# Taking the variances of a four-layer graph network from ScalarE squares, and starting the last six batches ahead

## The chip, the cores and the metric

The kernel runs on one core of one Trainium2 chip. The metric is the device time of one execution in microseconds (us). Before the change the median of the first three runs is 3364.07 us (3363.28 to 3366.58).

Short names: PE is TensorE's matmuls, PEld its weight loads, DVE is VectorE, ACT is ScalarE, POOL is GpSimd. "L198" is line 198 of the kernel in question; the change shifts most lines by 3 to 16, so one operation has two numbers (the product is L195 before and L198 after; query-key matmuls are L442 and L445, value products' transposing matmuls L619 and L629, the copy of their result oT L628 and L638). prT is the result of layer 3's softmax, written to DRAM (p_d) by one DMA transfer and read back, rearranged, by another; "half clock" is a granted TensorE clock of 0.50 in a stretch.

## The reference, cut to what matters

Four layers run over 128 independent batches, each a 128 x 512 tile. Each layer ends in a residual addition and a normalisation, and layer 3 has one more normalisation inside, so that a batch has five:

```python
def _layernorm(x, axis=-1, eps=1e-5):
    m = jnp.mean(x, axis=axis, keepdims=True)
    v = jnp.var(x, axis=axis, keepdims=True)
    return (x - m) / jnp.sqrt(v + eps)

x = _layernorm(x + adj @ x @ W0 + bias0)                       # layer 0
x = _layernorm(x + elu(softmax(e(x)) @ (x @ W1) + beta * ...)) # layer 1, masked graph attention
x = _layernorm(x + max over neighbours(...))                   # layer 2
# layer 3: 8 heads of masked attention, o = attention @ w_proj + b_proj
ln = (o - mu) * rsqrt(var + eps) * gamma + beta
x = _layernorm(x + o + ln)
```

The four lines for the layers are abbreviated; `_layernorm` is the reference's own.

## The kernel before

All instructions are issued by one program in a static order. A class `Plan` decides that order when the kernel is built: each batch is a chain of steps, each step names its engine and an assumed duration, and the plan always issues next the step that could start earliest by its own bookkeeping. Ties go to urgent steps, then to the lower rank. On the chip every engine worked through its queue in that order: in the trace of this kernel the 2304 instructions of ScalarE, the 5263 of VectorE and the 1027 of GpSimd start in the order of the built program, line for line, and so do PE's 1045 runs of matmuls of one line.

```python
    def use(self, engine, work, take=None, late=0.05, urgent=False):
        names = take if callable(take) else lambda: (take,) if take else ()
        return engine, work, names, late, not urgent
    ...
    def run(self):
        while self.requests:
            t, _, _, n = min(
                (self.at(r), r["want"][4], r["rank"], n) for n, r in enumerate(self.requests)
            )
            ...
            self.free[engine] = t + work
            self.now = r["ready"] = t + work + late
```

The normalisation takes mean and variance on VectorE, and 1/sqrt as a power on GpSimd:

```python
    def mean_rstd(src):
        yield use("DVE", 1.0)
        st = small.tile([P, 6], F32, name="st")
        nc.vector.bn_stats(st, src)
        mv = small.tile([P, 2], F32, name="mv")
        nc.vector.bn_aggr(mv, st)
        ve = small.tile([P, 1], F32, name="ve")
        nc.vector.tensor_scalar(ve, mv[:, 1:2], EPS, None, op0=ALU.add)
        yield use("POOL", 0.65, late=0.1, urgent=True)
        rstd = small.tile([P, 1], F32, name="rstd")
        nc.gpsimd.tensor_tensor(rstd, ve, neghalf, op=ALU.pow)
        return mv, rstd
```

The end of a batch's layer 3, and the ranks:

```python
        yield use("ACT", 0.6, urgent=True)
        oT = buf([P, K, P], "oT")
        nc.scalar.copy(oT, p)
        give(ba)
        bp = yield use("PE", 3.5, "mm", late=0.2)
        p = product(lambda k: oT[:, k, :], lambda k: wproj_sb[:, k, :])
        give(bo)
        bo = yield use("DVE", 0.69, "o", urgent=True)
        o = buf([P, D], "o")
        nc.vector.tensor_tensor(o, p, bproj_sb, op=ALU.add)
        give(bp)
        yield biased
        added = Event()
        plan.start(pool_add(xb, o, added), i)      # xb += o on GpSimd
        mv, rstd = yield from mean_rstd(o)
        yield added
        yield use("DVE", 1.65)
        ...                                        # two multiply-adds on DVE
        yield from layernorm_dve(xb)
        ...
        for i in range(NB):
            plan.start(batch(i), i if i < NB - 4 else i - 16)
        plan.run()
```

So the last four of the 128 batches run 16 ranks ahead, and others end the kernel.

## Time and profile before

| | before |
|---|---|
| median of three runs | 3364.07 us |
| profiled span | 3366.0 us |
| PE busy | 3324.6 us (99%) |
| DVE / ACT busy | 2669.9 / 1189.7 us (79% / 35%) |
| PE idle in the first 200 us | 7.9 us |
| PE idle from 200 to 3000 us | 7.7 us |

A busy time is the union of an engine's instructions. The last two rows are a stretch's length less PE's busy time in it. The granted TensorE clock was 1.00 from 200 to 3000 us. The profile's lines are in the prediction below; where they show a bracket such as `[5.99 <-DMA prT<-p_d]`, the engine was idle for 5.99 us before the instruction, until the named transfer landed.

### The profile page before, as it was taken

How to read it: one execution, taken by the hardware profiler on the slowest of the kernel's cores; microseconds unless marked ns; L12 is line 12 of the kernel's file. 1: busy time of each engine (PE TensorE's matmuls, PEld its weight loads, DVE VectorE, ACT ScalarE, POOL GpSimd, SP SyncE). 2: the span in 40 equal slices, each digit the busy share in tenths (PEclk: the TensorE clock that was granted, in tenths of full speed). 3: DMA queues.
4: the chain of work that ended last, by engine and by line, in shares of the span. 5: the costliest groups of instructions: out<-in, count | busy, mean ns of one | idle time of the engine just before them, and what ended most of it. 6: DMA issues, size and time to landing. Idle time of an engine off the chain costs nothing.

```text
span 3366.0 us, 43501 instructions
## 1 busy us (share of the span) xinstructions
PE 3324.6 (99%) x14729; PEld 2070.5 (62%) x14729; DVE 2669.9 (79%) x5527; ACT 1189.7 (35%) x3457; POOL 923.1 (27%) x1031
## 2 busy tenths in 40 slices
PE   9999999999999999999999999999999999999987
PEld 5665656566565666566656656665656665666655
DVE  7878786886978878877877886887887787788775
ACT  3433333333233334343333333333333333333332
POOL 2322221331322312312322331232232232232221
PEclk9999999999999999999999999999999999999999
DMA  4332323223232323222232322232322323232222
GB/s 157 98 103 63 104 75 93 69 80 113 68 99 76 97 79 91 94 79 82 79 109 66 100 85 91 85 89 83 91 85 82 98 73 97 76 94 88 69 82 75
DMA packets 458191, 296.01 MB, mean 88 GB/s; under 512 B 315888, under 2 KB 389744, under 8 KB 457968
## 3 DMA queue, kind: packets, MB, share of 16 engines
q1 hardware_dynamic: 457968, 293.23, 29.0%
q8 instruction: 117, 1.92, 0.2%
q14 instruction: 106, 0.87, 0.1%
HBM read 150.54 MB, written 142.61 MB: 87 GB/s over the span
## 4 chain that ended last, share of the span: by engine, by line
PE 90%; DVE 6%; DMA 2%; issue 1%; SPq 0%; ACT 0%; POOL 0%; POOLq 0%; DVEq 0%; ACTq 0%
PE mm L195 47%; PE mm L442 27%; PE tr L203 6%; PE sc L572 4%; PE tr L619 4%; PE mm L543 3%; DVE st L161 1%; DMA p_d<-pt 1%; DMA prT<-p_d 1%; DVE scr L516 1%; DVE x L648 1%; PE tr L383 0%; SPq L486 0%; DVE t L645 0%; DVE x L182 0%
## 5 line engine op out<-in xcount | busy, mean ns | idle before, releaser
L442 PE MATMUL mm<-xT,wqkv_sb 128*128 128x256 f32 x4096 | 918.2, 381 | 8.8 <-DVE st L161 8.8
L195 PE MATMUL mm<-w_sb,yT 128*128 128x512 f32 x2048 | 913.9, 596 | 2.3 <-ACT yT L206 2.3
L442 PEld LDWEIGHTS mm<-xT,wqkv_sb 128*128 128x128 f32 x4096 | 771.4, 190 | 138.3 <-issue 20.6
L168 POOL TENSOR_TENSOR rstd<-ve,neghalf 128x1 f32<-128x1 f32 x640 | 406.6, 635 | 1100.6 <-DVE ve L165 996.9
L195 PEld LDWEIGHTS mm<-w_sb,yT 128*128 128x128 f32 x2048 | 383.3, 191 | 453.3 <-issue 441.6
L188 POOL TENSOR_TENSOR x<-x,o 128x512 f32<-128x512 f32 x128 | 175.9, 1374 | 1128.3 <-DVE o L636 1117.6
L195 PE MATMUL mm<-wqkv_sb,xT 128*128 128x512 f32 x1024 | 464.4, 596 | 0.0
L195 PE MATMUL mm<-wproj_sb,oT 128*128 128x512 f32 x1024 | 460.9, 598 | 1.8 <-ACT oT L628 1.8
L590 ACT ACTIVATE pr<-pr,nmx 128x128 f32<-128x128 f32 x1024 | 397.6, 391 | 176.1 <-DVE nmx L586 174.6
L161 DVE BATCH_NORM_STATS2 st<-x 128x6 f32<-128x512 f32 x512 | 348.1, 680 | 3.1 <-ACT x L550 1.9
L579 DVE TENSOR_TENSOR pr<-sc,maskb 128x1024 f32<-128x1024 f32 x128 | 156.3, 1221 | 218.8 <-PE sc L572 218.0
L195 PEld LDWEIGHTS mm<-wproj_sb,oT 128*128 128x128 f32 x1024 | 191.8, 191 | 223.6 <-issue 214.4
L177 ACT ACTIVATE x<-x,nmr,rstd 128x512 f32<-128x512 f32 x256 | 205.0, 810 | 351.6 <-DVE nmr L175 326.9
L195 PEld LDWEIGHTS mm<-wqkv_sb,xT 128*128 128x128 f32 x1024 | 189.6, 190 | 199.0 <-issue 191.4
L206 ACT COPY yT<-tr 128x512 f32<-128x512 f32 x256 | 146.8, 582 | 263.9 <-PE tr L203 263.6
L188 POOL TENSOR_TENSOR x<-x,beta_sb 128x512 f32<-128x512 f32 x128 | 167.1, 1307 | 177.1 <-DVE xt L556 131.2
L516 DVE SCALAR_TENSOR_TENSOR scr<-x,wa_rows 128x512 f32<-128x512 f32 x256 | 200.4, 783 | 15.5 <-ACT x L177 10.2
L468 ACT COPY v<-mm 128x512 f32<-128x512 f32 x128 | 74.9, 585 | 347.7 <-PE mm L195 347.5
L450 ACT ACTIVATE qkT<-mm 128x512 f32<-128x512 f32 x128 | 76.1, 594 | 341.2 <-PE mm L442 341.0
L590 ACT ACTIVATION_READ_ACCUMULATOR pr<-pr,nmx 128x1 f32 x1024 | 193.1, 189 | 0.0
L188 POOL TENSOR_TENSOR x<-x,bias_sb 128x512 f32<-128x512 f32 x128 | 182.6, 1436 | 32.9 <-PE tr L203 22.9
L182 DVE TENSOR_SCALAR x<-x,mv,rstd 128x512 f32<-128x512 f32 x256 | 172.5, 676 | 14.4 <-POOL rstd L168 14.0
(63 smaller groups left out, 3558.6 us busy)
## 6 DMA issues: line engine op xcount, KB each, us to landing
p_d<-pt SPq DMA_DIRECT2D x128, 512.0 KB, 2.6
prT<-p_d SPq DMA_DIRECT2D x128, 512.0 KB, 3.8
x<-in_x SPq DMA_DIRECT2D x128, 256.0 KB, 2.9
x_d<-xt SPq DMA_DIRECT2D x128, 256.0 KB, 2.0
xT<-x_d SPq DMA_DIRECT2D x512, 64.0 KB, 2.5
out<-x SPq DMA_DIRECT2D x128, 256.0 KB, 2.0
e_d<-et SPq DMA_DIRECT2D x64, 128.0 KB, 1.7
eT<-e_d SPq DMA_DIRECT2D x64, 128.0 KB, 2.2
```

Source lines behind the costliest of these rows:

```text
L161: nc.vector.bn_stats(st, src)
L168: nc.gpsimd.tensor_tensor(rstd, ve, neghalf, op=ALU.pow)
L177: nc.scalar.activation(xb, xb, AF.Identity, bias=nmr, scale=rstd)
L182: nc.vector.tensor_scalar(xb, xb, mv[:, 0:1], rstd, op0=ALU.subtract, op1=ALU.mult)
L188: nc.gpsimd.tensor_tensor(dst, dst, other, op=ALU.add)
L195: nc.tensor.matmul(p, lhs(k), rhs(k), start=(k == 0), stop=(k == K - 1))
L203: nc.tensor.matmul(p[:, k, :], xb[:, k * P : (k + 1) * P], nodes, start=True, stop=True)
L206: nc.scalar.copy(yT, p)
L442: nc.tensor.matmul(p[:, j, :], wqkv_sb[:, k, (c + j) * P : (c + j + 1) * P], gr.xT[:, k, :], start=(k == 0), stop=(k == K - 1),)
L516: nc.vector.scalar_tensor_tensor(scr, xb, 1.0, wa_rows[:, j, :], op0=ALU.mult, op1=ALU.mult, accum_out=gr.s[:, b, j : j + 1],)
L579: nc.vector.tensor_tensor(pr, sc.rearrange("p j c m -> p (j c) m"), maskb[:, None, :].to_broadcast([P, H, P]), op=ALU.add,)
L590: nc.scalar.activation(pr[:, j, :], pr[:, j, :], AF.Exp, bias=nmx[:, j : j + 1], accum_out=sums[:, j : j + 1],)
```

## The change

The intent is to move the variance of all 640 normalisations from VectorE to ScalarE, which had two thirds of its time free (35% busy). The sum of a row now comes from an accumulator of the operation that writes the row, VectorE makes the negated mean of it, ScalarE squares the row about that mean and accumulates. Besides, six last batches run 12 ranks ahead, in place of four by 16. Cut to its core:

```diff
-    def mean_rstd(src):
-        yield use("DVE", 1.0)
-        st = small.tile([P, 6], F32, name="st")
-        nc.vector.bn_stats(st, src)
-        mv = small.tile([P, 2], F32, name="mv")
-        nc.vector.bn_aggr(mv, st)
+    def mean_rstd(src, total):
+        yield use("DVE", 0.15)
+        nm = small.tile([P, 1], F32, name="nm")
+        nc.vector.tensor_scalar(nm, total, -1.0 / D, None, op0=ALU.mult)
+        yield use("ACT", 1.0)
+        square = one.tile([P, D], F32, name="square")
+        var = small.tile([P, 1], F32, name="var")
+        nc.scalar.activation(square, src, AF.Square, bias=nm, accum_out=var)
+        yield use("DVE", 0.15)
         ve = small.tile([P, 1], F32, name="ve")
-        nc.vector.tensor_scalar(ve, mv[:, 1:2], EPS, None, op0=ALU.add)
+        nc.vector.tensor_scalar(ve, var, 1.0 / D, EPS, op0=ALU.mult, op1=ALU.add)
 ...
-        nc.vector.tensor_tensor(xb, p, xb, op=ALU.add)
+        nc.vector.scalar_tensor_tensor(
+            xb, p, 1.0, xb, op0=ALU.mult, op1=ALU.add, accum_out=total
+        )
 ...   (likewise with accum_out at the other four places that write a row to be normalised)
-                plan.start(..., g * G + 2 * h - (16 if g * G >= NB - 4 else 0))
+                plan.start(..., g * G + 2 * h - (12 if g * G >= NB - 6 else 0))
 ...   (likewise for the query-key steps)
-            plan.start(batch(i), i if i < NB - 4 else i - 16)
+            plan.start(batch(i), i if i < NB - 6 else i - 12)
```

More of the change, by code (lines that the diff above doesn't have):

```diff
@@ L168, in mean_rstd, with layernorm_act, layernorm_dve @@
         nc.gpsimd.tensor_tensor(rstd, ve, neghalf, op=ALU.pow)
-        return mv, rstd
-    def layernorm_act(xb):
-        mv, rstd = yield from mean_rstd(xb)
+        return nm, rstd
+    def layernorm_act(xb, total):
+        nm, rstd = yield from mean_rstd(xb, total)
         yield use("DVE", 0.21)
         nmr = small.tile([P, 1], F32, name="nmr")
-        nc.vector.tensor_scalar(nmr, mv[:, 0:1], rstd, -1.0, op0=ALU.mult, op1=ALU.mult)
+        nc.vector.tensor_tensor(nmr, nm, rstd, op=ALU.mult)
         yield use("ACT", 0.81)
         nc.scalar.activation(xb, xb, AF.Identity, bias=nmr, scale=rstd)
-    def layernorm_dve(xb):
-        mv, rstd = yield from mean_rstd(xb)
+    def layernorm_dve(xb, total):
+        nm, rstd = yield from mean_rstd(xb, total)
         yield use("DVE", 0.67)
-        nc.vector.tensor_scalar(xb, xb, mv[:, 0:1], rstd, op0=ALU.subtract, op1=ALU.mult)
+        nc.vector.tensor_scalar(xb, xb, nm, rstd, op0=ALU.add, op1=ALU.mult)
     def pool_add(dst, other, event, after=None):
@@ L369, in group @@
             for h in range(G // 2):
-                plan.start(attention1(groups[g], h), g * G + 2 * h - (16 if g * G >= NB - 4 else 0))
+                plan.start(attention1(groups[g], h), g * G + 2 * h - (12 if g * G >= NB - 6 else 0))
             for n in range(K):
-                plan.start(query_key(groups[g], n // 2 * 2 + K * (n % 2)), g * G + n / K - (16 if g * G >= NB - 4 else 0))
+                plan.start(query_key(groups[g], n // 2 * 2 + K * (n % 2)), g * G + n / K - (12 if g * G >= NB - 6 else 0))
         return groups[g]
@@ L507, in batch @@
         yield biased
-        yield use("DVE", 0.69, urgent=True)
-        nc.vector.tensor_tensor(xb, p, xb, op=ALU.add)
+        yield use("DVE", 0.78, urgent=True)
+        total = small.tile([P, 1], F32, name="total")
+        nc.vector.scalar_tensor_tensor(
+            xb, p, 1.0, xb, op0=ALU.mult, op1=ALU.add, accum_out=total
+        )
         give(bp)
-        yield from layernorm_act(xb)
+        yield from layernorm_act(xb, total)
         yield wa_ready
@@ L532, in batch @@
         nc.scalar.activation(ex, p, AF.Exp)
-        yield use("DVE", 1.5, urgent=True)
+        yield use("DVE", 1.6, urgent=True)
+        total = small.tile([P, 1], F32, name="total")
         nc.vector.scalar_tensor_tensor(xb, p, 0.0, xb, op0=ALU.max, op1=ALU.add)
-        nc.vector.scalar_tensor_tensor(xb, ex, 1.0, xb, op0=ALU.min, op1=ALU.add)
+        nc.vector.scalar_tensor_tensor(
+            xb, ex, 1.0, xb, op0=ALU.min, op1=ALU.add, accum_out=total
+        )
         give(bp)
         give(be)
-        yield from layernorm_act(xb)
+        yield from layernorm_act(xb, total)
         bp = yield use("PE", 0.95, "mm", late=0.2, urgent=True)
@@ L548, in batch @@
         give(bp)
-        yield use("ACT", 0.81)
-        nc.scalar.activation(xb, xb, AF.Identity, bias=mx)
-        yield from layernorm_dve(xb)
+        yield use("ACT", 0.92)
+        total = small.tile([P, 1], F32, name="total")
+        nc.scalar.activation(xb, xb, AF.Identity, bias=mx, accum_out=total)
+        yield from layernorm_dve(xb, total)
         bt = yield use("DVE", 0.65, "xt")
@@ L633, in batch @@
         give(bo)
-        bo = yield use("DVE", 0.69, "o", urgent=True)
+        bo = yield use("DVE", 0.78, "o", urgent=True)
         o = buf([P, D], "o")
-        nc.vector.tensor_tensor(o, p, bproj_sb, op=ALU.add)
+        total = small.tile([P, 1], F32, name="total")
+        nc.vector.scalar_tensor_tensor(
+            o, p, 1.0, bproj_sb, op0=ALU.mult, op1=ALU.add, accum_out=total
+        )
         give(bp)
@@ L640, in batch @@
         plan.start(pool_add(xb, o, added), i)
-        mv, rstd = yield from mean_rstd(o)
+        nm, rstd = yield from mean_rstd(o, total)
         yield added
-        yield use("DVE", 1.65)
+        yield use("DVE", 1.75)
         t1 = one.tile([P, D], F32, name="t1")
         nc.vector.scalar_tensor_tensor(
-            t1, o, mv[:, 0:1], gamma_sb, op0=ALU.subtract, op1=ALU.mult
+            t1, o, nm, gamma_sb, op0=ALU.add, op1=ALU.mult
         )
-        nc.vector.scalar_tensor_tensor(xb, t1, rstd, xb, op0=ALU.mult, op1=ALU.add)
+        total = small.tile([P, 1], F32, name="total")
+        nc.vector.scalar_tensor_tensor(
+            xb, t1, rstd, xb, op0=ALU.mult, op1=ALU.add, accum_out=total
+        )
         give(bo)
-        yield from layernorm_dve(xb)
+        yield from layernorm_dve(xb, total)
         yield use("SP", 0.1, late=3.0)
```

## The prediction

> **What bounds the kernel now.** I read the page's busy list first, then PE's waits, then PE in order of time and stretch by stretch through head and tail, then the groups of instructions that the change touches. The busy list:
>
> ```profile
> PE 3324.6 (99%) x14729; PEld 2070.5 (62%) x14729; DVE 2669.9 (79%) x5527; ACT 1189.7 (35%) x3457; POOL 923.1 (27%) x1031
> ```
>
> 99% could flatter, since a matmul's end is modelled, so I check PE by its rate: in the chain of waits eight 512-column instructions (one product) take 3.43 us wherever they stand in a dense stretch, and sixteen 256-column ones 3.46. Between 200 and 3000 us PE was busy 2792.32 of 2800 us. TensorE is the bound there and its clock is full; at most 7.7 us of gaps can be won in the middle. What is left is in the gaps at both ends. PE's waits, longest first:
>
> ```profile
> PE mm L442 <- DVE st L161: 8.8, 1, 8.8
> PE tr L619 <- DMA prT<-p_d: 7.9, 6, 6.0
> PE tr L203 <- DMA x<-in_x: 3.0, 2, 2.0
> PE tr L308 <- DMA adj_sb<-in_adj: 2.7, 1, 2.7
> PE tr L383 <- DVE scr L516: 2.7, 4, 1.0
> ```
>
> (engine, line and tile, what it waited for, total us, times, longest). PE in order of time shows where the two largest are (start, us, instruction, idle before):
>
> ```profile
> 3278.04 16.80 PE L442 MATMUL mm<-xT,wqkv_sb 128*128 128x256 f32 x64 [8.79 <-DVE st L161]
> ...
> 3336.59 1.09 PE L619 MATMUL tr<-prT,v 128*64 128x128 f32 x16
> 3338.70 3.70 PE L195 MATMUL mm<-wproj_sb,oT 128*128 128x512 f32 x8 [1.02 <-ACT oT L628]
> 3348.39 1.98 PE L619 MATMUL tr<-prT,v 128*64 128x128 f32 x16 [5.99 <-DMA prT<-p_d]
> 3351.09 5.77 PE L195 MATMUL mm<-wproj_sb,oT 128*128 128x512 f32 x8 [0.73 <-ACT oT L628]
> ```
>
> Both are in the last 100 us. The second column shows a second cost: 64 instructions took 16.80 us after the 8.79 us gap, against 14.01 elsewhere; 8 took 5.77 after the 5.99 us gap, against 3.6 to 3.7. The stretches show the granted clock (first fraction after POOL's field):
>
> ```profile
> 3265.00:3270.00 5.00, 4.25 (x10) 1.52 (x8) 4.86 (x11) 0.16 (x1) 3.89 (x5) 1.00 0.17 59
> 3270.00:3275.00 5.00, 0.00 (x0) 0.00 (x0) 4.78 (x7) 0.00 (x0) 3.30 (x3) 0.84 0.46 103
> 3275.00:3280.00 5.00, 1.96 (x5) 1.64 (x6) 4.72 (x13) 0.00 (x0) 2.09 (x4) 0.50 0.47 106
> 3280.00:3285.00 5.00, 5.00 (x17) 4.08 (x16) 3.06 (x7) 0.48 (x1) 3.56 (x4) 0.64 0.41 157
> ```
>
> So removable tail cost: 8.8 + 2.8 (first gap and its slow restart) and 6.0 + 2.1 + 0.9 (last gap, its slow product and its slow tr): 20.6 us. After PE's last matmul (3356.9) 9.1 us remain for the last normalisations and the store.
>
> [...] the last softmax's exps ended at 3332.5, but its reciprocal stood behind the bias add of another batch and ran at 3335.0. [...]
>
> **The change part by part.** The groups that carry the costs (busy us, mean ns):
>
> ```profile
> L161 DVE BATCH_NORM_STATS2 st<-x 128x6 f32<-128x512 f32 x512 | 348.1, 680 | 3.1 <-ACT x L550 1.9
> L163 DVE BATCH_NORM_AGGREGATE mv<-st 128x2 f32<-128x6 f32 x640 | 116.4, 182 | 22.1
> L165 DVE TENSOR_SCALAR ve<-mv 128x1 f32<-128x1 f32 x640 | 98.3, 154 | 22.2
> L550 ACT ACTIVATE x<-x,mx 128x512 f32<-128x512 f32 x128 | 92.4, 722 | 167.9 <-DVE mx L547 165.7
> L590 ACT ACTIVATION_READ_ACCUMULATOR pr<-pr,nmx 128x1 f32 x1024 | 193.1, 189 | 0.0
> L516 DVE DVE_READ_ACCUMULATOR scr<-x,wa_rows 128x1 f32 x256 | 20.8, 81 | 0.0
> ```
>
> 1. *DVE.* Removed: 640 statistics (348.1 us for 512, 87.6 for the other 128) and 640 aggregates (116.4): 552 us. Added: 640 negated means at the 154 ns of a 128x1 tensor_scalar, 99 us; four of the five sums per batch come from a DVE accumulator, 512 x 81 ns = 41 us; two of those ops become scalar_tensor_tensor, which on PSUM costs the same 684 ns as the 682 and 686 of the adds they replace. Net about -412 us: DVE 2670 to about 2260 (67%). All of it lies beside PE.
>
> 2. *ACT.* 640 squares at 722 + 189 ns = 583 us, and 128 accumulator reads, 24 us: 1190 to about 1800 (54%). Also beside PE. The built program still holds one table load.
>
> 3. *Latency of one normalisation.* Before: 0.68 + 0.18 + 0.15 with hops, 1.1 us on DVE. After: accumulator read 0.08, mean 0.15, square and read 0.9, 0.15, and two crossings between engines at 0.05 to 0.1: 1.4 to 1.5 us. Hidden in the middle; at the end two stand in a row behind the last product: +0.9 us.
>
> 4. *Rank.* Four last batches 16 ranks ahead become six, 12 ahead. Its worth is read from the built order of PE. Before, only two products (6.9 us) stand between the last four neighbour-max matmuls (L543) and the query-key block that needs those batches transposed; that is the 8.8 us gap. After, two groups of two are separated: between the last pair's maxima and its query-key block stand one tr, two products, 48 query-key instructions, a value product and scores: 1.0 + 6.9 + 10.5 + 3.4 + 1.1 = 23 us. The chain (max, add, normalise, transpose, two DMAs) I add up to about 17.5 us with the new latencies and the DVE queue as ordered. So the 8.8 us gap and its 2.8 us restart vanish: -11.6 us.
>
> 5. *Last softmax.* From the last value products on, PE's order is the same. DVE's is not: after the reciprocal and multiply the transposition follows with only one 0.15 us op between, where before 5 us of others' work stood ahead of it (reciprocal 3335.0, transposition 3340.5). By the durations above it starts at about 3335.7 on the old time scale, 4.8 us earlier, and prT (2.6 + 3.9 us of DMA) lands at 3343.4 instead of 3348.3. [...] the copy oT of the third batch now stands behind a square that waits for DVE's whole update of another batch, which I put at 3340.3. Its product starts at 3341.0 instead of 3338.7, and the last tr follows it at 3344.5. Last product about 3346.3 to 3349.8 at full clock, against 3356.9; the 3.4 us gap may still cost 1 to 2 us of half clock. With +0.9 us of latency the part is worth -4.5 us.
>
> 6. *Head.* The DMA waits (5.7 us) stay. DVE loses a fifth of its load there, so the L383 waits (2.7 us, of which 1.9 in the head) mostly go: -1 us. PE changes from 64-row work (L572, L619) to other work 225 times instead of 219, each about 0.2 us (3.63 against 3.43): +1 us.
>
> Sum: -11.6 - 4.5 - 1 + 1 = -16 us; 3364.07 becomes 3348. In the middle I take the gaps as unchanged.
>
> **Rivals.** (a) *Unloading DVE speeds the whole kernel.* DVE at 79% looks near the limit, and 412 us off it tempts. Against it: PE's gaps in 2800 us of middle are 7.7 us. It would need a PE bound by waits; the gain is capped there at 7.7 us (3340). (b) *ACT becomes the new wait.* Every PSUM copy that frees PE's banks now queues behind squares of 0.9 us. For it: [...] the case found in step 5. Against it: ACT stays at 54%, three mm banks each have 3.4 us of product as slack, and the schedule accounts 1.0 us for a square. If one batch in four lost 0.3 us, 10 us would go and the result be 3358. (c) *The tail only trades gaps*: six batches together wait for each other's attention transfers, and a gap of 5 us with its slow restart appears elsewhere: 3356. [...]
>
> **Range and chances.** Best case (both gaps gone, middle gaps halved, no slow restart): 3364 - 20.6 - 4 = 3339. Worst likely case, (b) or (c): 3359. A 2% gain is 67 us, more than all idle time of PE (41 us): 1%. A 2% loss needs 67 us of new waits in a schedule with slack on ACT: 2%.
>
> **What would show it.** Right: the L442 wait of 8.8 us gone, no stretch near half clock before the last 30 us; DVE near 2260 and ACT near 1800 with a PE busy time within 5 us; squares near 720 ns plus 190; in the last 30 us, oT behind a square, PE waiting for ACT about 3 us. Wrong: waits of L198 on ACT copies all through the middle (b); a new gap over 3 us at L445 or at the tr of eT in the last 100 us (c); PE busy clearly below 3310, which would mean that its rate depends on the neighbours after all.

## The result

The change takes the median to 3350.88 us (3350.37 to 3351.51, four runs); in the same rounds the kernel before had a median of 3365.32 us. The ratio is 0.9957, with a 95% interval of 0.994 to 0.9975: the same within 2%, and a small gain beyond doubt. A ratio here is the mean time of one kernel's runs over that of the other's in the same rounds, so not quite the ratio of the medians. Both kernels were profiled (granted clock 0.996 and 0.998).

The busy list of the kernel after, in the form of the first line in the prediction:

```profile
PE 3320.5 (99%) x14729; PEld 2065.4 (62%) x14729; DVE 2282.3 (68%) x5399; ACT 1676.8 (50%) x4865; POOL 914.6 (27%) x1031
```

VectorE lost 388 us, ScalarE gained 487, PE stayed within 4.1. PE's waits after (engine, line, tile, what it waited for; total us, times, longest):

```profile
PE mm L198 <- ACT oT L638: 6.0, 3, 4.4
PE tr L386 <- DVE scr L522: 5.0, 5, 1.8
PE tr L206 <- DMA x<-in_x: 3.2, 2, 2.3
PE tr L311 <- DMA adj_sb<-in_adj: 2.7, 1, 2.7
PE tr L629 <- DMA prT<-p_d: 1.1, 2, 0.7
```

The 8.8 us wait of the query-key block is gone, and 7.9 us for prT are down to 1.1. In their place PE waits for the copy oT on ScalarE. PE in order of time near the end (start, us, instruction, idle before):

```profile
3280.02 3.60 PE L198 MATMUL mm<-wqkv_sb,xT 128*128 128x512 f32 x8
...
3321.93 1.09 PE L629 MATMUL tr<-prT,v 128*64 128x128 f32 x16
3327.44 6.69 PE L198 MATMUL mm<-wproj_sb,oT 128*128 128x512 f32 x8 [4.42 <-ACT oT L638]
...
3335.84 3.70 PE L198 MATMUL mm<-wproj_sb,oT 128*128 128x512 f32 x8 [0.68 <-ACT oT L638]
```

A single gap of 4.42 us is left, and the product behind it takes 6.69 us in place of 3.6. ScalarE in the same time shows what the copy stood behind:

```profile
3326.11 0.72 ACT L165 ACTIVATE square<-o,nm 128x512 f32<-128x512 f32 x1 [5.77 <-DVE nm L161]
3326.73 0.19 ACT L165 ACTIVATION_READ_ACCUMULATOR square<-o,nm 128x1 f32 x1
3326.83 0.56 ACT L638 COPY oT<-tr 128x512 f32<-128x512 f32 x1
```

ScalarE stood idle for 5.77 us ahead of a square that waited for VectorE, with the copy ready behind it for the last 3 us (its input, written by the matmuls that begin at 3321.93, was there at 3323.02). And VectorE was late there; VectorE and GpSimd in order of time:

```profile
3319.38 1.27 POOL L191 TENSOR_TENSOR x<-x,o 128x512 f32<-128x512 f32 x1 [40.32 <-DVE o L647]
3319.64 2.10 DVE L607 TENSOR_TENSOR pr<-pr,rs 128x1024 f32<-128x1024 f32 x1
```

The softmax's multiplication took 2.10 us, where the median of its 128 is 1.225. I come back to it below.

The 16.3 us between the two profiled spans split as follows. "Group start" is where the value product of the last pair of batches begins (3294.68 us before, 3280.02 after).

| part | before | after | difference |
|---|---|---|---|
| PE idle, 0 to 200 us | 7.9 | 6.9 | -1.0 |
| PE idle, 200 to 3000 us | 7.7 | 6.1 | -1.5 |
| gap before the query-key block, and its slow restart | 8.8 + 2.8 | 0 | -11.6 |
| group start to the end | 71.3 | 69.7 | -1.6 |

The four make -15.7; the rest is not told apart.

### The profile page after: what moved, and what is told of

It reads as the page before. It is cut to its first block, busy times and chain, and to the rows that moved or that the text cites. A ratio compares the mean times of both kernels' runs of the same rounds, so it can differ in the third digit from the quotient of the medians.

```text
span 3349.7 us, 45044 instructions
## 1 busy us (share of the span) xinstructions
PE 3320.5 (99%) x14729; PEld 2065.4 (62%) x14729; DVE 2282.3 (68%) x5399; ACT 1676.8 (50%) x4865; POOL 914.6 (27%) x1031
## 4 chain that ended last, share of the span: by engine, by line
PE 93%; DVE 4%; DMA 1%; ACT 1%; issue 1%; POOL 0%; SPq 0%; POOLq 0%; DVEq 0%; ACTq 0%
PE mm L198 49%; PE mm L445 26%; PE tr L206 6%; PE sc L582 4%; PE tr L629 4%; PE mm L552 3%; DVE scr L522 1%; PE tr L386 0%; DVE x L542 0%; DVE x L185 0%; ACT x L180 0%; DVE xt L566 0%; DVE x L662 0%; DVE x L541 0%; DVE mx L555 0%
## 5 line engine op out<-in xcount | busy, mean ns | idle before, releaser
L171 POOL TENSOR_TENSOR rstd<-ve,neghalf 128x1 f32<-128x1 f32 x640 | 395.2, 626 | 1320.4 <-DVE ve L168 1104.6
L165 ACT ACTIVATE square<-x,nm 128x512 f32<-128x512 f32 x512 | 367.7, 718 | 181.6 <-DVE nm L161 158.5
L522 DVE SCALAR_TENSOR_TENSOR scr<-x,wa_rows 128x512 f32<-128x512 f32 x256 | 213.1, 832 | 39.6 <-ACT x L180 34.2
L185 DVE TENSOR_SCALAR x<-x,nm,rstd 128x512 f32<-128x512 f32 x256 | 161.1, 631 | 73.8 <-POOL rstd L171 72.2
L165 ACT ACTIVATE square<-o,nm 128x512 f32<-128x512 f32 x128 | 92.2, 720 | 232.3 <-DVE nm L161 217.0
```

What stands on the lines that cost most here:

```text
L165: nc.scalar.activation(square, src, AF.Square, bias=nm, accum_out=var)
L185: nc.vector.tensor_scalar(xb, xb, nm, rstd, op0=ALU.add, op1=ALU.mult)
L522: nc.vector.scalar_tensor_tensor(scr, xb, 1.0, wa_rows[:, j, :], op0=ALU.mult, op1=ALU.mult, accum_out=gr.s[:, b, j : j + 1],)
```

## The experiments

The theory is the prediction's: the ranks remove the query-key gap, the squares only rearrange the end, and the middle does not care about VectorE's load because PE is full there. The rivals are that the freed VectorE is what helps, and that ScalarE's added work costs something throughout. Each kernel of these was correct on the chip, and each had four executions.

### e0_after_again

The changed kernel without an edit, as the base of what follows.

> The changed kernel unaltered, as the base for the other runs on the same chip. Both theories: 3351 us, within 3 us. In the profile one gap of PE of 4 to 5 us before a projection product in the last 30 us, waiting for the ScalarE copy oT, and no gap at the query-key block.

Measured: 3351.70 us (3351.44 to 3352.45), ratio 0.9954 [0.9938, 0.9971]. The result repeats.

### e1_rank_only

The kernel before, with the new ranks and nothing else.

```diff
-            plan.start(batch(i), i if i < NB - 4 else i - 16)
+            plan.start(batch(i), i if i < NB - 6 else i - 12)
```

(and the same in the two places of the groups)

> Old variance (statistics on VectorE), new ranks (six batches, 12 ahead). Theory A (the order of the last batches is the whole gain, the squares only move work beside PE): at least the full gain, 3343 to 3351 us; no gap at the query-key block (8.8 us before), no copy behind a square, the built order puts the last transposition right after its multiply. Rival B (the gain comes from the 388 us taken off VectorE): 3362 to 3366 us, with VectorE near 2670 us busy.

Measured: 3352.94 us (3351.88 to 3353.61), ratio 0.9957 [0.9942, 0.9972], with VectorE still at 2664.2 us. That is 13.8 us under the kernel before (3366.7 in these rounds), and 2 us above the theory's range. PE in order of time:

```profile
3260.48 1.09 PE L619 MATMUL tr<-prT,v 128*64 128x128 f32 x16 [3.04 <-DMA prT<-p_d]
3261.50 15.77 PE L442 MATMUL mm<-xT,wqkv_sb 128*128 128x256 f32 x64
...
3337.49 3.70 PE L195 MATMUL mm<-wproj_sb,oT 128*128 128x512 f32 x8 [0.74 <-ACT oT L628]
```

With the old normalisation, the ranks remove both end gaps, the one of 8.8 and the one of 6.0, with all three slow restarts: 8.8 + 2.8 + 6.0 + 2.1 + 0.9 = 20.6 us. They open four smaller gaps shortly ahead, between 3249 and 3260 us, of 0.67, 0.68, 0.59 and 3.04 us, and a slow block behind the last of them (15.77 against 14.01): 6.7 us. 20.6 less 6.7 is 13.9, beside 13.8 between the medians; the sum is not the whole account, since the stretch behind PE's last matmul grew from 9.1 to 10.6 us. So most of the gain is the ranks', with VectorE as loaded as ever.

### e2_square_only

The changed kernel with the old ranks.

```diff
-            plan.start(batch(i), i if i < NB - 6 else i - 12)
+            plan.start(batch(i), i if i < NB - 4 else i - 16)
```

> Squares on ScalarE, old ranks (four batches, 16 ahead). Theory A: most of the gain is missing, 3354 to 3362 us; the built order leaves only one value product and one score block of PE work beside the last softmax of the last two batches, so I expect a gap of some 10 us there with a slow restart, in place of the two gaps of before. Rival B (VectorE load): the full gain, 3348 to 3353 us, with VectorE near 2280 us busy.

Measured: 3362.99 us (3362.61 to 3365.93), ratio 0.9989 [0.9974, 1.0004]. The profiled execution is the longest of the four. The squares alone are worth 3.7 us of median, which the interval does not tell from nothing. PE in order of time:

```profile
3234.93 5.38 PE L445 MATMUL mm<-xT,wqkv_sb 128*128 128x256 f32 x16 [2.36 <-DMA x_d<-xt]
...
3339.18 1.98 PE L629 MATMUL tr<-prT,v 128*64 128x128 f32 x16 [12.61 <-DMA prT<-p_d]
3341.83 6.67 PE L198 MATMUL mm<-wproj_sb,oT 128*128 128x512 f32 x8 [0.67 <-ACT oT L638]
```

The 8.8 us gap is gone here also, since the static order came out otherwise, but a gap of 12.61 us stands at the last softmax. 16.6 us of gap and slow restart there (12.61 + 0.9 + 3.1) and 4.1 further up (2.36 + 1.8) replace the 20.6 of before. In the same rounds the ranks alone give -13.8, the squares alone -3.7, and both together -15.0 us: the parts make 17.5, 2.5 more than both together, which the intervals do not tell apart.

### e5_copy_first

The changed kernel, in which the plan is told to hold two negated means back (3 us later by its bookkeeping), so that the copy oT comes ahead of their squares in ScalarE's queue.

```diff
-        nm, rstd = yield from mean_rstd(o, total)
+        nm, rstd = yield from mean_rstd(o, total, 3.0 if i == 119 else 0.05)
...
-        yield from layernorm_dve(xb, total)
+        yield from layernorm_dve(xb, total, 3.0 if i == 118 else 0.05)
```

> The changed kernel with one thing moved: in the last four batches the copy oT stands ahead of the squares of batches 118 and 119 in ScalarE's queue. If the 4.4 us gap and the slow product after it (6.7 us instead of 3.7) come from that square: gap under 1 us, product near 3.7 us, then a wait of about 2 us for the last softmax's transfer, total 3344 to 3348 us. If something else holds the copy (VectorE's slow multiply, the transfer), the gap stays and the time is 3350 to 3352.

Measured: 3349.21 us (3347.67 to 3351.93), ratio 0.9947 [0.9932, 0.9962]: 1.2 us above the expected range, and 2.5 us under the changed kernel in the same rounds, with ranges that overlap. The profiled execution is the fastest of the four. PE in order of time:

```profile
3323.63 3.70 PE L198 MATMUL mm<-wproj_sb,oT 128*128 128x512 f32 x8 [0.74 <-ACT oT L638]
3329.49 1.09 PE L629 MATMUL tr<-prT,v 128*64 128x128 f32 x16 [2.15 <-DMA prT<-p_d]
```

The gap of 4.42 us is down to 0.74, and the product behind it is back at 3.70 us. PE's order is the same as in the changed kernel, instruction for instruction; VectorE's differs in 15 places, ScalarE's in 6 and GpSimd's in 2, all at the end. So the square in front of the copy is the cause of that gap. Not all of that (3.7 us of gap and 3.0 of slow product) comes out of the time, because the last softmax becomes what is waited for (2.15 us for prT; the multiplication of 2.10 us lies on its path), and the stretch behind PE's last matmul grows from 10.2 to 10.9 us.

### e6_tail_mixed

On e5, the old statistics on VectorE for the layer-3 normalisations of the two batches that end last, to test whether their latency sets the end.

```diff
+            nm, rstd = yield from (mean_rstd_dve(o) if i in (120, 121) else mean_rstd(o, total, ...))
```

> Copy-first kernel, and in the last two batches (120, 121) layer 3's two variances by the old statistics on VectorE, without the crossings to ScalarE. If the longer latency of a normalisation costs at the end, the stretch from the last product's end to the end of the program falls from 10.9 us to 9.5 to 10.3, and the time is 0.5 to 1.5 us under the copy-first kernel's 3349; if the queue order decides there, no change.

Measured: 3349.94 us (3348.07 to 3351.53), ratio 0.9948 [0.9933, 0.9963]. No gain over e5, and the stretch from PE's last matmul to the end is 10.96 us, where e5 has 10.94: taking ScalarE out of the last two batches' normalisations moves nothing that these runs can see.

### e7_add_later

On e5, GpSimd's residual addition of batch 118 is held until its 1/sqrt is done, so that it no longer runs beside the softmax's multiplication.

```diff
-        plan.start(pool_add(xb, o, added), i)
+        held = Event()
+        plan.start(pool_add(xb, o, added, held if i == 118 else None), i)
         nm, rstd = yield from mean_rstd(o, total, 3.0 if i == 119 else 0.05)
+        done(held)
```

> Copy-first kernel with one GpSimd add (batch 118's residual) held back until after that batch's reciprocal root, so that it does not run beside VectorE's softmax multiply of batch 121. If the two engines get in each other's way, the multiply takes 1.22 us instead of 2.10, the wait for the last softmax's transfer falls from 2.2 to about 1.3 us and the total by 0 to 1 us; if the 2.10 us has another cause, it stays.

Measured: 3346.89 us (3346.50 to 3347.38), ratio 0.994 [0.9923, 0.9957]. VectorE, then PE, in order of time:

```profile
3320.02 1.22 DVE L607 TENSOR_TENSOR pr<-pr,rs 128x1024 f32<-128x1024 f32 x1
...
3329.10 1.09 PE L629 MATMUL tr<-prT,v 128*64 128x128 f32 x16 [1.26 <-DMA prT<-p_d]
```

The multiplication is back at 1.22 us, and the wait for prT shrank from 2.15 to 1.26, by as much as VectorE lost before (0.88). PE's order is that of e5, and so is VectorE's as far as the transposition behind the multiplication; the edit reordered VectorE in 19 places after that, ScalarE in 3 and GpSimd in 4. Before, addition and multiplication lay side by side: in the changed kernel the addition ran from 3319.38 to 3320.65, the multiplication began at 3319.64, so 1.01 us of it lay beside the addition, and it took 0.88 us longer than its median. The median of the total fell by 2.3 us against e5, where 0 to 1 had been expected; the profiled spans differ by 1.2, so the rest is not explained. This is the fastest kernel: it beats the kernel before by 0.6% and the changed kernel (e0, in other rounds) by 4.8 us, with ranges that do not touch.

### e3_dve_reload

The changed kernel with a dead statistics instruction on VectorE behind every negated mean; nothing reads its result. VectorE is as loaded as before, while the plan, which makes the order, is not told.

```diff
         nc.vector.tensor_scalar(nm, total, -1.0 / D, None, op0=ALU.mult)
+        st = small.tile([P, 6], F32, name="st")
+        nc.vector.bn_stats(st, src)
```

> The changed kernel with the old statistics instruction put back as dead work behind each negated mean (640 of them, about 436 us on VectorE), every engine's order otherwise unaltered. Theory A (VectorE's load lies beside TensorE): VectorE near 2720 us busy, more than before the change, and the time within 3 us of the changed kernel, 3350 to 3355 us. Rival B (the gain is VectorE's relief): back to 3360 to 3366 us, with new waits of TensorE for VectorE in the middle.

Measured: 3390.59 us (3389.33 to 3393.32), ratio 1.0071 [1.0054, 1.0088]. The theory missed by 35 us or more, and the rival's range by 24. VectorE has 2609.1 us, less than the kernel before (about 2720 had been expected), and still PE waits in many places. PE's waits:

```profile
PE mm L554 <- ACT x L182: 8.7, 12, 1.7
PE tr L388 <- DVE scr L524: 7.9, 7, 2.3
PE mm L200 <- ACT oT L640: 6.5, 3, 4.4
PE tr L631 <- DMA prT<-p_d: 5.5, 4, 2.4
```

Taken alone this run would speak for the rival "VectorE's load is what counts". But e1 carries 2664 us on VectorE without such waits. PE, ScalarE and GpSimd have the changed kernel's order here. The two runs differ, among other things, in whether the plan had counted the load; e8 tests that.

### e8_dve_planned

e3, with the load counted.

```diff
-        yield use("DVE", 0.15)
+        yield use("DVE", 0.85)
         nm = small.tile([P, 1], F32, name="nm")
```

> The changed kernel with the same dead statistics after every negated mean as in e3_dve_reload, but now counted (0.85 us instead of 0.15 for that step) by the bookkeeping that makes the static order of the queues. VectorE about 2609 us busy, as there. Theory A (the 39 us that the dead statistics cost came from an order made for a VectorE with gaps that were no longer there, not from the load): the waits of the middle go, 3350 to 3360 us, PE idle between 200 and 3200 us under 12 us. Rival B (the load itself, or its place between the mean and the variance, is what TensorE waits for): 3380 to 3393 us as without the bookkeeping, PE idle in that stretch over 22 us.

Measured: 3373.30 us (3372.56 to 3373.87), ratio 1.0017 [1.0001, 1.0034], between the two ranges: neither total was right. The stretches tell why. First e3, then e8, from 200 to 3200 us (PE, PEld, DVE, ACT and POOL busy):

```profile
200.00:3200.00 3000.00, 2970.84 (x13161) 1843.13 (x13160) 2326.01 (x5378) 1498.61 (x4359) 815.78 (x914) 1.00 0.28 85
```

```profile
200.00:3200.00 3000.00, 2995.68 (x13293) 1863.19 (x13294) 2330.77 (x5433) 1523.61 (x4436) 819.40 (x926) 1.00 0.29 87
```

With the same load on VectorE, PE was idle for 29.2 us in e3 and for 4.3 in e8 (7.1 in the changed kernel over the same stretch). VectorE has 2582.6 us in all. So the middle's waits came from an order made for another VectorE, not from the load. The total is long because of two gaps near the end. PE of e8 in order of time:

```profile
3307.68 16.70 PE L447 MATMUL mm<-xT,wqkv_sb 128*128 128x256 f32 x64 [11.84 <-DMA xT<-x_d]
...
3346.31 1.97 PE L631 MATMUL tr<-prT,v 128*64 128x128 f32 x16 [12.69 <-DMA prT<-p_d]
3348.96 6.19 PE L200 MATMUL mm<-wproj_sb,oT 128*128 128x512 f32 x8 [0.68 <-ACT oT L640]
```

Two gaps of 24.5 us in all, in front of the query-key block and at the last softmax, where the kernel before had its own.

### e10_dve_planned_ranks

e8 with the old ranks, to see whether the end gaps belong to the load or to the order.

```diff
-            plan.start(batch(i), i if i < NB - 6 else i - 12)
+            plan.start(batch(i), i if i < NB - 4 else i - 16)
```

> e8_dve_planned (dead statistics, counted by the bookkeeping) with the old ranks, four last batches 16 ahead, in place of six 12 ahead. In the built order of PE the last query-key block of that version again has products and value products of other batches between its parts, where e8 had it as one block of 64 instructions behind its own pair's maxima. Theory A (the waits of the middle are settled by the bookkeeping, and which end gap is left is chance of the order, which the ranks move): the gaps of 11.8 and 12.7 us at the end of e8 shrink to under 6 us in all, VectorE about 2600 us, 3347 to 3358 us. Rival B (a VectorE load of 77% itself makes the end late, whatever the ranks): 3366 to 3376 us, with end gaps of over 15 us in all.

Measured: 3365.80 us (3362.08 to 3365.96), ratio 0.9994 [0.9978, 1.0011]. Both totals missed, the rival's by 0.2 us only, and the two gaps make 13.9 us, where the theory had under 6 and the rival over 15. The gap of 12.69 us is down to 2.21; the other stayed, at an earlier place:

```profile
3279.02 16.58 PE L447 MATMUL mm<-xT,wqkv_sb 128*128 128x256 f32 x64 [11.66 <-DMA xT<-x_d]
```

I had read only the last rows of the built order, which looked well mixed, and not the ones 60 us further up, where the block of 64 stands right behind the neighbour maxima that it depends on. So the ranks moved one of the two gaps. Whether a VectorE at 77% could do without the other under this normalisation stays open; e1 does without it at 79%, with the old normalisation.

### e4_act_double

The changed kernel with every square taken twice, the second into a dead tile, the plan not told.

```diff
         nc.scalar.activation(square, src, AF.Square, bias=nm, accum_out=var)
+        square2 = one.tile([P, D], F32, name="square2")
+        var2 = small.tile([P, 1], F32, name="var2")
+        nc.scalar.activation(square2, src, AF.Square, bias=nm, accum_out=var2)
```

> The changed kernel with every square done twice (the second one dead): ScalarE from 1677 to about 2140 us busy. Theory A (ScalarE has slack in the middle, pays only in the tail): 3352 to 3362 us, most of it in the last 30 us, where the copy oT waits for two squares instead of one and each of the last two normalisations is up to 0.9 us longer. Rival C (ScalarE is about to be the wait that took the place of the one removed): over 3375 us, with waits of TensorE for ScalarE copies all through the middle.

Measured: 3374.01 us (3373.46 to 3374.33), ratio 1.002 [1.0005, 1.0035], with ScalarE at 2085.0 us (62%): between the two ranges, and 1 us under the rival's. PE was idle for 19.3 us from 200 to 3200 us, with waits on ScalarE spread over the whole of it.

### e9_act_planned

e4, with the second square counted.

```diff
-        yield use("ACT", 1.0)
+        yield use("ACT", 1.95)
```

> The changed kernel with the second dead square of e4_act_double, now counted (1.95 us instead of 1.0 for the squaring step). ScalarE about 2085 us busy (62%). Theory A (ScalarE has room for still more as long as the order is made for it): 3350 to 3360 us, PE idle between 200 and 3200 us under 12 us. Rival B (a first-in-first-out queue with 62% of work makes PE's copies late whatever the order): 3368 us or more, idle in that stretch over 17 us.

Measured: 3356.30 us (3355.08 to 3357.41), ratio 0.9966 [0.9951, 0.9981]; as the theory had it. ScalarE has 2103.2 us (63%), and PE was idle for 5.0 us from 200 to 3200 us. The largest gap left is one near the end again:

```profile
3270.94 16.29 PE L448 MATMUL mm<-xT,wqkv_sb 128*128 128x256 f32 x64 [9.21 <-DMA xT<-x_d]
```

A copy oT behind squares costs another 2.90 us at the end. So the middle had room for twice the squares on ScalarE, if the order is made for them; the whole is 4.6 us slower than the changed kernel (e0, in other rounds).

## Why the prediction was right, point by point

The time was right: 3348 predicted in 3339 to 3359, and 3350.9 measured (-16 us predicted, -14.4 in the same rounds). In part it was luck: the sum gives the ranks 11.6 of the 16 us and counts 4.5 apart for the last softmax, while e1 has 13.8 from the ranks alone, by another set of gaps. By its steps:

1. *DVE, -412 predicted, -388 measured.* Right in kind. The small operations were cheaper (145 ns in place of 154), but the product of mean and 1/sqrt took 322 ns where it had been 202 (256 of them, +31 us), and the softmax's multiplication averaged 1372 ns in place of 1226 (+19 us). I had left out that these ran longer beside some of GpSimd's instructions. e7 shows it for one instance of the multiplication, and the changed kernel's trace for the averages: the 96 multiplications with no GpSimd instruction beside them took at most 1.228 us, and all 22 that took over 1.3 us had one that had begun before them, in 20 cases the residual addition. Of the products of mean and 1/sqrt, the 165 without took at most 0.163 us, and all 46 over 0.17 us had one.

2. *ACT, about 1800 predicted, 1676.8 measured.* The durations were right (718 to 720 and 188 ns), and the sum of all 640 is 580 us. But the busy time rose by 487 only: an accumulator read overlapped the instruction behind it by 0.09 us (the copy above begins at 3326.83, while the read runs from 3326.73 to 3326.92). Adding durations overcounts a union.

3. *Latency, +0.9 us at the end.* The size came out, but not for the reason given. From PE's last matmul to the end of the span it was 9.1 us before and 10.2 after, +1.1. Yet with the squares and the old ranks it is 9.5 (e2), with the old statistics and the new ranks 10.6 (e1), and the old statistics in the last two batches change nothing (e6). So the squares' latency alone is worth some 0.4 us (e2), and the rest goes with the order. The step's own figures, 1.1 us before and 1.4 to 1.5 after, twice over, make 0.6 to 0.8, not 0.9. Of its two crossings, put at 0.05 to 0.1 us each, the one back from ScalarE took 0.03 us in the changed kernel's trace (accumulator read to variance, 3326.92 to 3326.95), the one to ScalarE mostly 0.03 to 0.09.

4. *Ranks, -11.6.* Right in size: the gap and its restart are gone. But they are not the ranks' alone: with the old ranks the squares' order removes that gap too, and puts one of 12.61 us at the last softmax (e2). What I had not seen either is that the ranks alone also remove the last softmax's gap, as e1 showed, and open others (3.04 us and a slow block) that the squares then close. The two halves of the change were less apart than steps 4 and 5 told them.

5. *Last softmax, -4.5 predicted, -1.6 measured.* The mechanism was right, the copy oT behind a square, and e5 showed it by undoing it. Two terms of the sum were mis-sized. I put the gap at 3.4 us, and it was 4.42: VectorE came late, with 0.88 us lost in the multiplication and 0.80 in the update of x (1.55 in place of 0.75). And I gave the half clock 1 to 2 us, an estimate, where the product took 3.1 longer (6.69 against 3.6, with a granted clock of 0.50 from 3327 to 3333 us). With 1.5 us for the half clock these two make 2.6 of the 2.9 us between predicted and measured.

6. *Head and middle, 0 in all, -2.5 measured.* The head's -1.0 is as predicted. In the middle I had taken the gaps as unchanged, and they shrank by 1.5. The waits of L386 did not mostly go: they fell from 1.6 (the prediction has 1.9) to 0.8 in the first 80 us, but rose from 2.7 to 5.0 in the whole. VectorE's score product ahead of them, L522, waited 34.2 us for ScalarE's normalised rows, and only 10.2 before: the longer latency of step 3 shows in the middle too, where I had called it hidden. That it is the squares agrees with e1, where these waits stay at 2.7. The +1 us for 225 row changes can't be seen.

Of the rivals, (a), a kernel sped up by a lighter VectorE, is refuted: e1 has 13.8 of the 15.0 us with VectorE unchanged, and e8 puts the load back with no more waits in the middle. For the end it is not settled: e8 and e10, with VectorE at 77% under the new normalisation, both keep a gap of 11.7 to 11.8 us. (b), ScalarE as the new wait, holds in the changed kernel in one place only, at the end; e9 doubled the squares with 5.0 us of idle PE in the middle. (c), a tail that only trades gaps, is what most of the experiments that touch the order did, e2, e8, e9 and e10 among them; it did not come in the changed kernel itself, whose order happened to be a good one. That it would be good could be read beforehand only from the built order, as step 4 did.

What failed was not the prediction but my belief behind it, that in the middle load is free. e3 and e4 missed by it. Load is free there as far as the plan knows of it: 327 us more on VectorE cost 39 us uncounted; counted (300 us in the trace), they left PE no more idle in the middle than the changed kernel has it, and the 22 us that they still cost are at the end, where the two gaps make 24.5.

## What to carry to other kernels

On a kernel whose main engine is 99% busy, moving work between the other engines gains little by itself (3.7 us in e2); read the few gaps at the ends, and count each with the slow work that may follow (3.1 us behind the gap of 4.42 us here). In a statically ordered kernel give the scheduler the true duration of every new operation, since the same work cost 39 us uncounted and 22 counted on VectorE (e3, e8), and 22 and 5 on ScalarE (e4, e9), and look at the built order of the last 100 us after every edit, because an edit of its steps or ranks can reshuffle it. Where a short copy that the main engine waits for stands in one engine's queue behind work that waits for a third engine, let the copy go first (e5: the gap of 4.42 us became 0.74).

## What the traces showed of the clock, the accumulator reads and VectorE beside GpSimd

- The clock around gaps of PE. In the gap of 8.79 us before the change the granted clock fell while PE stood (0.84 in the prediction's stretch without a matmul, 0.50 in the next). Around the gap of 4.42 us of the changed kernel it was 0.83 from 3326 to 3327 us, without a matmul, and 0.50 from 3327 to 3333. Stretches at 0.50 followed shorter gaps as well: one of 2.36 us (e2, sixteen 256-column instructions took 5.38 us instead of 3.6) and one of 2.21 us followed by one of 0.68 (e10, 0.50 from 3346 to 3352 us, a product of 6.22 us). Slow work followed gaps of 2.90 us (a product of 5.40 us in e9) and 3.04 us (e1, 15.77 instead of 14.01), where the clock was not read in stretches this fine. Behind those of 2.15 us (e5, granted clock 1.00 from 3325 to 3337 us) and 2.19 us (e6), each followed by one of some 0.7, a product took 3.70 us. In e2 the clock was 1.00 until 3234 us, and then a mean of 0.80 over 2 us with 0.50 behind it; if it went from 1.00 straight to 0.50, that is, by estimate, half clock for the last 0.8 us, from about 3235.2 on, after PE had started again at 3234.93 (the granted clock is the first fraction after POOL's field):

```profile
3234.00:3236.00 2.00, 1.07 (x3) 0.97 (x4) 1.85 (x5) 0.00 (x0) 2.00 (x3) 0.80 0.72 266
3236.00:3238.00 2.00, 2.00 (x6) 1.56 (x5) 1.88 (x5) 0.21 (x1) 1.73 (x2) 0.50 0.42 67
```

- The squares took 718 to 720 ns, where the prediction had 722 from L550. The accumulator read behind each took 188 ns, with some 0.1 us of it under the next instruction.
- The accumulator read on VectorE is an instruction of its own in the traces: 0.08 us.
- The softmax's multiplication of 1.225 us became 2.10 beside 1.01 us of a GpSimd addition, and was 1.22 with the addition held back (e7).
- Work that the static order did not count: 39 us for 327 us on VectorE (e3), 22 us for 408 us on ScalarE (e4).
